# The last half of a decoder kernel: token pairs through the feed-forward one by one, hidden units on partitions

## The chip, the cores and the metric

The kernel runs on one core of a Trainium2 chip. The metric is the device time of one execution in microseconds (us); "before" is the median of three runs, 2210.0 us (2209.04 to 2211.79). The engines are named as the profile names them: PE multiplies matrices (PEld is its loading of weights), DVE and ACT work element by element and can read PE's result memory PSUM, [...]and SP, ACT and POOL have queues on which they issue DMAs.

## The reference

One decoder layer on x of 4 x 1024 tokens x 512 features, all in float32: a gated self-attention within the sequence, a cross-attention to a context of 4 x 1024 x 384, and a feed-forward, each behind a layer norm and added to x. What the change touches is the feed-forward:

```python
s = jnp.einsum('btd,dm->btm', x, Win) + bin_            # 512 -> 64 channels
h = jax.nn.relu(s[..., None] * W1 + b1)                 # 16 hidden units for each channel
g = jnp.einsum('btmh,mh->btm', h, W2) + b2              # back to 64
out = jnp.einsum('btm,md->btd', g, Wout) + bout         # 64 -> 512
...
x = x + _L0_ffn_ref(_layernorm(x, axis=-1), ...)
```

Each of the 64 channels has a small network of its own with 16 hidden units.

## The kernel before

The work is cut into units: a phase (self-attention, then cross-attention) times a batch row, eight units in order, and each unit into two halves of 512 tokens, that is four tiles of 128 tokens. `attention(u, hf)` gives the 32 score steps of a half (four groups of heads times eight tiles of keys): PE forms scores in PSUM (L574), ACT exponentiates (L579), DVE adds up for the denominators (L587), PE multiplies with the values (L601). `beside(u, hf)` gives the list of other work, and `run` deals it out between the score steps by the weights written beside each part. So the order of instructions on every engine is written out by hand; the only things decided elsewhere are the waits between engines.

The other work for a half comes from `post(u, hf)`: output projection (`project`, L87 through the helper `columns`, which makes four products of 32 columns each that fill the array side by side), residual add (L770), layer norm (`root`, `norm`), and, in the second phase, the feed-forward. There the normalized rows are turned so that features lie on partitions, multiplied with Win (`inputs`, L841), and then `hidden(h)` goes through the 16 hidden units: the 64 channels of the first two tiles (pair 0) lie on partitions 0 to 63, those of the other two (pair 1) on partitions 64 to 127, and for each unit ACT makes one relu of 128 x 256 (L858) and DVE one multiply-and-add into g (L864). `outputs(t)` multiplies with Wout (L875), adds the residual on DVE (L881) and stores a tile (L883).

The feed-forward of a half is dealt out beside the attention of the next one. The last half of the last unit has no next one. Its work, and the rest of the half before it, stand behind the loop in an order of their own: `settle` makes the last denominators on PE and divides (L719, L720), the projection's parts come as `o[0]` to `o[7]` (`o[2t]` three quarters of tile t, `o[2t+1]` the last quarter), and

```python
go(o[1], o[3], *o[4:6], *sum(held[0]["out"], []), ln[0], *ln[2:4], *o[6:8], b[0], *tr[0:2], s[0])
go(ln[1], *ln[4:6], b[1], *tr[2:4], s[1])
...
h = sum(tail["h"], [])
go(*h[0:4])
...
go(*h[4:], *sum(tail["out"], []))
```

`held[0]["out"]` are the outputs of the half before, `ln` roots and norms, `tr` the turning of a tile by PE (`across`, L325), `s[k]` the product with Win for a pair, `b` (L892) puts the bias bout into PSUM ahead of the outputs, and `h` are the 16 hidden units. PSUM is shared out by pools: `bank()` has two buffers of one bank (f), the score tiles s two of two banks, and av and sm are one bank each. Weights of 1 MB live in three buffers (w), the exponentiated tiles in six (e). A flag that says whether the fast path was numerically safe is computed from `marks` (L723, L724, L1063 to L1070); at the end each engine reads it (L59) and branches.

## Time and profile before

| | us |
|---|---|
| median of the runs before | 2210.0 |
| the profiled execution, its own time | 2212.4 |
| its span, first to last instruction | 2210.6 |
| last score product of the loop | about 2151 |
| last add on DVE ends | 2204.6 |
| last store's issue ends | 2204.95 |

| engine | busy us | share |
|---|---|---|
| PE | 2174.1 | 98% |
| DVE | 1562.2 | 71% |
| ACT | 1238.5 | 56% |
| POOL | 82.0 | 4% |

In the lines that follow in the prediction, a line of the chain has the start, the duration, the engine, what it writes and the source line; a line of the timeline has start and duration, engine, line, operation, what is written from what, shapes and count, and in brackets how long the engine stood idle before and what ended that. In the table of stretches come the stretch and its length, busy time and number of instructions of PE, PEld, DVE, ACT and POOL, then the clock granted to PE, the share of the DMA engines and GB/s. A float32 product appears as two records.

### The profile page before, as it was taken

To read this page: it belongs to the slowest core of one execution; us is meant where nothing else is said; L and a number is where in the kernel's file an instruction comes from. 1 tells how busy PE (TensorE), PEld (TensorE's weight loads), DVE (VectorE), ACT (ScalarE), POOL (GpSimd) and SP (SyncE) were. 2 spreads that over 40 slices of the span, in tenths; PEclk is the share of its full clock that TensorE was granted. 3 is DMA by queue.
4 is the path that set the end of the run, shared out by engine and by line. 5 is a ranking of instruction groups with operands and counts; after the bars stand their busy time and mean duration, and the time that the engine had idled before them with its cause. 6 is when DMAs were issued, how large, how long until landed. Compare 5 with 4: busy or idle time off the path is not lost.

```text
span 2210.6 us, 52746 instructions
## 1 busy us (share of the span) xinstructions
PE 2174.1 (98%) x22598; PEld 547.7 (25%) x22598; DVE 1562.2 (71%) x2526; ACT 1238.5 (56%) x1489; POOL 82.0 (4%) x118
## 2 busy tenths in 40 slices
PE   8999999999999999999999999999999999999995
PEld 3322222222222222222222222222222222222222
DVE  4478675796757957577686666877787777856476
ACT  0155545555455554555556565676757566667673
POOL 1000000030300000000000000000000000000000
PEclk9999999999999999999999999999999999999998
DMA  4412123032230211211232132312233142303031
GB/s 142 132 56 63 55 98 106 24 88 66 100 106 25 85 66 55 79 37 51 60 89 89 45 87 64 101 60 65 58 98 87 60 97 64 88 12 117 21 88 40
DMA packets 153304, 161.70 MB, mean 73 GB/s; under 512 B 46202, under 2 KB 91898, under 8 KB 151908
## 3 DMA queue, kind: packets, MB, share of 16 engines
q1 hardware_dynamic: 149068, 156.14, 24.4%
q8 instruction: 179, 2.93, 0.6%
q0 software_dynamic: 2144, 0.98, 0.3%
q10 hardware_dynamic: 1848, 1.12, 0.2%
q14 instruction: 65, 0.53, 0.1%
HBM read 115.40 MB, written 42.74 MB: 72 GB/s over the span
## 4 chain that ended last, share of the span: by engine, by line
PE 92%; DVE 3%; issue 2%; DMA 2%; ACT 2%; SPq 0%; DVEq 0%; ACTq 0%
PE f L87 35%; PE s L574 24%; PE av L601 21%; PE sm L609 6%; PE sm L631 3%; DVE es L587 1%; ACT e L579 1%; PE f L875 1%; DMA xn<-rows_d 1%; DVE g L864 1%; PE f L841 1%; DMA rows_d<-r 0%; PE f L325 0%; PE f L471 0%; PE f L1025 0%
## 5 line engine op out<-in xcount | busy, mean ns | idle before, releaser
L579 ACT ACTIVATE e<-s 128x1024 f32<-128x1024 f32 x1024 | 993.7, 1022 | 713.2 <-PE s L574 518.0
L587 DVE TENSOR_TENSOR es<-es,e 128x1024 f32<-128x1024 f32 x534 | 642.3, 1227 | 255.8 <-ACT e L579 253.5
L574 PE MATMUL s<-q,k 32*64 32x512 f32 x8192 | 608.7, 614 | 4.5 <-ACT e L579 2.9
L601 PE MATMUL av<-e,v 128*32 128x512 f32 x4096 | 551.1, 604 | 0.0
L87 PE MATMUL f<-xT,w 128*32 128x512 f32 x2816 | 333.7, 592 | 0.6 <-PE f L87 0.6
L595 DVE SCALAR_TENSOR_TENSOR eg<-e,sw,eg 128x512 f32<-128x512 f32 x448 | 318.6, 747 | 2.3
L585 DVE TENSOR_TENSOR es<-e 128x1024 f32<-128x1024 f32 x89 | 106.7, 1222 | 221.0 <-ACT e L579 187.8
L574 PEld LDWEIGHTS s<-q,k 32*64 32x64 f32 x8192 | 133.1, 130 | 449.4 <-ACT e L579 243.3
L87 PE MATMUL f<-w,q 128*32 128x512 f32 x1984 | 240.5, 592 | 0.7 <-DVE q L720 0.7
L601 PEld LDWEIGHTS av<-e,v 128*32 128x32 f32 x4096 | 88.1, 108 | 404.6 <-issue 401.4
L87 PEld LDWEIGHTS f<-xT,w 128*32 128x32 f32 x2816 | 92.1, 110 | 211.3 <-issue 204.4
L609 PE MATMUL sm<-e,sw 128*2 128x512 f32 x1024 | 133.3, 592 | 0.0
L87 PE MATMUL f<-w,xT 128*32 128x512 f32 x896 | 106.0, 592 | 0.6 <-DVE q L284 0.6
L87 PEld LDWEIGHTS f<-w,q 128*32 128x32 f32 x1984 | 65.5, 110 | 150.0 <-issue 142.3
L858 ACT ACTIVATE hid<-sT,units 128x256 f32<-128x256 f32 x128 | 76.7, 605 | 31.1 <-DVE g L864 24.5
L87 PE MATMUL f<-w,ctxT 128*32 128x512 f32 x768 | 92.6, 592 | 0.0
L87 PE MATMUL f<-ctxT,w 128*32 128x512 f32 x768 | 92.3, 592 | 0.0
L778 POOL TENSOR_TENSOR r<-res,bo_bc 128x512 f32<-128x512 f32 x32 | 40.9, 1278 | 1040.5 <-DVE res L770 702.7
L631 PE MATMUL sm<-es,ones 128*1 128x512 f32 x348 | 65.8, 601 | 0.0
L864 DVE SCALAR_TENSOR_TENSOR g<-hid,units,g 128x256 f32<-128x256 f32 x120 | 57.7, 481 | 11.3 <-ACT hid L858 5.8
L770 DVE TENSOR_TENSOR res<-f,res 128x512 f32<-128x512 f32 x62 | 42.5, 686 | 17.9 <-PE f L87 8.9
L681 DVE TENSOR_TENSOR q<-both,recb 128x512 f32<-128x512 f32 x63 | 43.3, 687 | 7.5 <-DMA recb<-rec_d 7.5
(258 smaller groups left out, 1037.2 us busy)
## 6 DMA issues: line engine op xcount, KB each, us to landing
recb<-rec_d SPq DMA_DIRECT2D x252, 64.0 KB
xT<-rows_d SPq DMA_DIRECT2D x60, 256.0 KB
rows_d<-r SPq DMA_DIRECT2D x60, 256.0 KB
w<-in_xattn_Wo SPq DMA_DIRECT2D x9, 1024.0 KB
w<-wout_d SPq DMA_DIRECT2D x8, 1024.0 KB
res<-in_x SPq DMA_DIRECT2D x32, 256.0 KB
x1b_d<-r SPq DMA_DIRECT2D x32, 256.0 KB
res<-x1b_d SPq DMA_DIRECT2D x32, 256.0 KB
```

Of the source, the lines that this page charges most:

```text
L87: nc.tensor.matmul(to[r], lhsT=lhsT[:, j, :] if len(lhsT.shape) == 3 else lhsT[:, r], rhs=rhs, **flags)
L574: nc.tensor.matmul(s[m : m + 64, j, :], lhsT=k[r, g, kt * P + m : kt * P + m + 64], rhs=q[r, g, :], start=True, stop=True,)
L579: nc.scalar.activation(e, s, AF.Exp, scale=SCALE)
L585: nc.vector.tensor_tensor(me["es"][i], me["e", 0][i], es[i], ALU.add)
L587: nc.vector.tensor_tensor(me["es"][i], me["es"][i], es[i], ALU.add)
L595: nc.vector.scalar_tensor_tensor(eg, es[0][:, h, :], gate(kt), eg, ALU.mult, ALU.add)
L601: nc.tensor.matmul(av[r, :], lhsT=me["v"][:, kt, HG * g + h, :], rhs=es[h // 2][:, h % 2, :], start=(kt == 0), stop=(kt == NT - 1),)
L609: nc.tensor.matmul(sm[j * DH : j * DH + sums, :], lhsT=me["sw"][:, t, HG * g + 2 + h, :] if ph == 0 else ones, rhs=me["e", t][1][:, h, :], ...
L631: nc.tensor.matmul(sm[j * DH : j * DH + 1, :], lhsT=ones, rhs=e, start=True, stop=True)
L681: nc.vector.tensor_tensor(me["q", hf][:, g, :], both[:, 0, :], all_, ALU.mult)
L858: nc.scalar.activation(hid, res["s"], AF.Relu, bias=units[:, 1, h : h + 1], scale=units[:, 0, h : h + 1])
L864: nc.vector.scalar_tensor_tensor(res["g"], res["hid"], units[:, 2, h - 1 : h], res["g"], ALU.mult, ALU.add)
```

## The change

In the last half of the last unit the feed-forward is done for pair 0 and then for pair 1, with hidden units on partitions. There are 64 x 16 = 1024 of them, eight chunks of 128. A constant 0/1 matrix "spread" copies each channel to its 16 units by a product on PE (four products of 32 x 64 per pair of chunks, 256 columns), ACT or DVE applies w1, b1 and relu with per-partition operands (the first chunk of each two on ACT, the second on DVE in two passes, except in the last two, both on ACT), and a matrix "gather" with W2 folded in adds the 16 units up again on PE, into av for pair 0 and into sm for pair 1. The matrices are loaded into a weight buffer by four DMAs beside the first half of the last unit (`load_spread`), and W2 is folded in by one DVE pass beside the second half (`fold_w2`).

Besides, in the last half the residual enters the projection through PE, as a product with the identity (`keep`) ahead of the others; ACT then copies the sum to SBUF, and the statistics read PSUM. The outputs of the half before (`kept`) get their residual in the same way, and ACT copies them out. The bias bout is added to the rows on POOL, and no longer put into PSUM by products. A pair's outputs are two tiles: the first with an identity product and an ACT copy, stored from ACT's queue, the second with a DVE add, stored from SP's. The order behind the loop is written anew.

```diff
+        def load_spread():
+
+            w = wp.tile([P, NC, D], F32, tag="w", name="w").rearrange("p c d -> p (c d)")
+            k = NF * P
+            S["spread"] = w[:, 0:k].rearrange("p (c i) -> p c i", c=NF)
+            S["gather"] = w[:, k : k + NF * M].rearrange("p (c m) -> p c m", c=NF)
+            S["hidden"] = w[:, k + NF * M : k + NF * M + 3 * NF].rearrange("p (w c) -> p w c", w=3)
+            for i in range(2):
+                nc.sync.dma_start(S["spread"][i * M : (i + 1) * M], a["spread"])
+            nc.sync.dma_start(S["gather"], a["gather"])
+            nc.sync.dma_start(S["hidden"], a["units"])
+
+        def fold_w2():
+            w2 = S["hidden"][:, 2, :].unsqueeze(2).to_broadcast([P, NF, M])
+            nc.vector.tensor_tensor(S["gather"], S["gather"], w2, ALU.mult)
+
+        def networks(res, k, g):
+
+            nk = NF // 2
+            r = slice(k * M, (k + 1) * M)
+            cols = slice(0, 2 * P)
+            hid = {}
+
+            def spread(i):
+
+                s = ps.tile([P, 2, HALF], F32, tag="s", name="s")
+                for j in range(2):
+                    c, rows = i + nk * j, slice(k * M + j * DH, k * M + (j + 1) * DH)
+                    for m in range(0, P, 64):
+                        nc.tensor.matmul(
+                            s[m : m + 64, j, cols], lhsT=S["spread"][rows, c, m : m + 64], rhs=res["s"][rows, :],
+                            start=True, stop=True,
+                        )
+                for j in range(2):
+                    c = i + nk * j
+                    hid[c] = p4.tile([P, 2, HALF], F32, tag="e", name="e", bufs=6)[:, 0, cols]
+                    w1, b1 = (S["hidden"][:, w, c : c + 1] for w in range(2))
+                    if j and i < nk - 1:
+                        nc.vector.tensor_scalar(hid[c], s[:, j, cols], w1, b1, ALU.mult, ALU.add)
+                        nc.vector.tensor_scalar(hid[c], hid[c], 0.0, None, ALU.max)
+                    else:
+                        nc.scalar.activation(hid[c], s[:, j, cols], AF.Relu, bias=b1, scale=w1)
+
+            def gather(i):
+                for j in range(2):
+                    nc.tensor.matmul(
+                        g[k * M + j * DH : k * M + (j + 1) * DH, cols], lhsT=S["gather"][:, i + nk * j, ts(j, DH)],
+                        rhs=hid[i + nk * j], start=(i == 0), stop=(i == nk - 1),
+                    )
+
+            def summed():
+                nc.scalar.activation(res["g"][r, :], g[r, cols], AF.Identity, bias=fb[r, 1:2])
+
+            return spread, gather, summed
...
+            kept = (u, hf) == (len(order) - 1, 0)
...
+            def keep(t, to):
+
+                nc.tensor.matmul(to, lhsT=ident, rhs=res[t], start=True, stop=False)
...
+                            if cs[0] == 0:
+                                keep(t, res["po"])
                         for c in cs:
                             columns(
                                 res["po"], me["q", hf][:, c, ts(t, P)], me["wo", hf][:, c, :],
-                                start=(c == 0), stop=(c == NC - 1),
+                                start=(c == 0 and not last), stop=(c == NC - 1),
...
-                        r = res[t]
-                        nc.vector.tensor_tensor(r, res["po"], r, ALU.add)
+                        r = res["po"] if last else res[t]
+                        if last:
+                            nc.scalar.copy(res[t], r)
+                        else:
+                            nc.vector.tensor_tensor(r, res["po"], r, ALU.add)
...
-                if not res.get("banks"):
-                    two = ps.tile([P, 2, HALF], F32, tag="s", name="s")
-                    res["banks"] = [two[:, i, :] for i in range(2)]
-                return res["banks"].pop(0)
+                return ps.tile([P, 2, HALF], F32, tag="s", name="s")[:, 0, :]
...
-                return lambda: nc.vector.tensor_tensor(res[t], res[t], bout_bc, ALU.add)
+                return lambda: (nc.gpsimd if last else nc.vector).tensor_tensor(res[t], res[t], bout_bc, ALU.add)
...
+            def pair_inputs(k):
+
+                def f():
+                    if k == 0:
+                        res["s"] = p2.tile([P, 2 * P], F32, tag="sT", name="sT", bufs=1)
+                        res["g"] = p2.tile([P, 2 * P], F32, tag="g", name="g", bufs=1)
+                    ss = bank()
+                    r = slice(k * M, (k + 1) * M)
+                    for c in range(NC):
+                        for m in range(2):
+                            nc.tensor.matmul(
+                                ss[k * M + m * DH : k * M + (m + 1) * DH, 0 : 2 * P],
+                                lhsT=win[:, c, m * DH : (m + 1) * DH], rhs=chunk(res["xn"], c, 2 * k, 2),
+                                start=(c == 0), stop=(c == NC - 1),
+                            )
+                    nc.scalar.activation(res["s"][r, :], ss[r, 0 : 2 * P], AF.Identity, bias=fb[r, 0:1])
+                return f
...
-                    po = res["bout", t] if last else [bank(), bank()]
+                    po = [bank(), bank()]
+                    for k in range(2):
+                        if kept:
+                            keep(2 * k + t, po[k])
                     for k in range(2):
                         nc.tensor.matmul(
                             po[k], lhsT=res["g"][k * M : (k + 1) * M, ts(t, P)], rhs=wout[k * M : (k + 1) * M, :],
-                            start=not last, stop=True,
+                            start=not kept, stop=True,
                         )
                     for k in range(2):
                         i = 2 * k + t
-                        nc.vector.tensor_tensor(res[i], po[k], res[i], ALU.add)
+                        if kept:
+                            nc.scalar.copy(res[i], po[k])
+                        else:
+                            nc.vector.tensor_tensor(res[i], po[k], res[i], ALU.add)
                         tt = 4 * hf + i
                         nc.sync.dma_start(out[b][tt * P : (tt + 1) * P, :], res[i])
...
-            def bout(t):
-
-                def f():
-                    po = res["bout", t] = [behind(), behind()]
-                    for k in range(2):
-                        r = slice(k * M, (k + 1) * M)
-                        nc.tensor.matmul(
-                            po[k], lhsT=share[r].to_broadcast([M, P]), rhs=bout_bc[r, :], start=True, stop=False
-                        )
-                return f
+            def pair_outputs(k):
+
+                two = ps.tile([P, 2, HALF], F32, tag="s", name="s")
+                r = slice(k * M, (k + 1) * M)
+                keep(2 * k, two[:, 0, :])
+                for t in range(2):
+                    nc.tensor.matmul(
+                        two[:, t, :], lhsT=res["g"][r, ts(t, P)], rhs=wout[r, :], start=t == 1, stop=True
+                    )
+                nc.scalar.copy(res[2 * k], two[:, 0, :])
+                nc.vector.tensor_tensor(res[2 * k + 1], two[:, 1, :], res[2 * k + 1], ALU.add)
+                for t, dma in enumerate((nc.scalar.dma_start, nc.sync.dma_start)):
+                    tt = 4 * hf + 2 * k + t
+                    dma(out[b][tt * P : (tt + 1) * P, :], res[2 * k + t])
...
+            if last:
+                r |= {"res": res, "outputs": pair_outputs}
...
-                "b": [[(2, bout(t))] for t in range(2)] if last else [[(0, biased(t))] for t in range(4)],
+                "b": [[(0, biased(t))] for t in range(4)],
                 "tr": [[(1 if last else 0, tr(t))] for t in range(4)],
-                "s": [[(2, inputs)]] if not last else [[(1, lambda k=k: inputs((k,)))] for k in range(2)],
+                "s": [[(2, inputs)]] if not last else [[(1, pair_inputs(k))] for k in range(2)],
...
+                else:
+                    out += one(load_spread)
                 out += pause(2) + weave(h[0:k], pause(10)) + weave(h[k:], last["o"]) + held.pop()["out"]
                 out += (ending[0]["load"] if hf else []) + weave(last["ln"], pause(5)) + last["xT"]
                 out += weave(last["b"], pause(8))
-                out += weave(last["tr"], pause(3)) + last["s"] + weave(some(last, 8), pause(14))
+                out += (one(fold_w2) if hf else []) + weave(last["tr"], pause(3)) + last["s"] + weave(some(last, 8), pause(14))
...
-        go(o[2], *h[0:3])
+        go(o[2], *h[0:3], o[4])
         for t in range(4):
             divide(t)
             go(*h[3 + 2 * t : 5 + 2 * t])
         S[n - 1]["divided", 1] = HG - 1
-        go(o[1], o[3], *o[4:6], *sum(held[0]["out"], []), ln[0], *ln[2:4], *o[6:8], b[0], *tr[0:2], s[0])
-        go(ln[1], *ln[4:6], b[1], *tr[2:4], s[1])
-
+        go(o[1], o[6], o[3], ln[0], o[5], o[7], *sum(held[0]["out"], []), *ln[2:4], *tr[0:2], s[0])
+        go(ln[1], *ln[4:6], *b)
+        spread, gather, summed = networks(tail["res"], 0, av)
+        spread(0)
+        spread(1)
+        go(tr[2])
+        gather(0)
+        spread(2)
+        go(tr[3])
+        gather(1)
+        spread(3)
+        gather(2)
+        gather(3)
+        summed()
 
         look()
         fine = p1.tile([P, 2 * NS + B * NT], F32, name="fine")
         nc.vector.tensor_scalar(fine, marks, LIM, None, ALU.is_le)
         least = p1.tile([P, 1], F32, name="least")
         nc.vector.tensor_reduce(least, fine, AX.X, ALU.min)
+        go(s[1])
+        tail["outputs"](0)
+        spread, gather, summed = networks(tail["res"], 1, sm)
+        spread(0)
+        spread(1)
+        gather(0)
+        spread(2)
+        gather(1)
+        spread(3)
         pn = bank()
         nc.tensor.matmul(pn[0:1, 0:1], lhsT=least, rhs=ones, start=True, stop=True)
-        h = sum(tail["h"], [])
-        go(*h[0:4])
+        gather(2)
+        gather(3)
+        summed()
         nc.vector.tensor_scalar(flag, pn[0:1, 0:1], P - 0.5, None, ALU.is_lt)
-        go(*h[4:], *sum(tail["out"], []))
+        tail["outputs"](1)
 
```

More of the change, by code (lines that the diff above doesn't have):

```diff
@@ L832, in tr, with inputs @@
                 return f if last else lambda: blocks(res["xn"], t)
-            def inputs(ks=(0, 1)):
-                if 0 in ks:
-                    res["ss"] = bank()
-                ss = res["ss"]
+            def inputs():
+                ss = bank()
                 for c in range(NC):
-                    for j in range(2 * ks[0], 2 * ks[-1] + 2):
+                    for j in range(4):
                         k, m = divmod(j, 2)
@@ L845, in inputs @@
                         )
-                if 1 not in ks:
-                    return
                 sT = p2.tile([P, 2 * P], F32, tag="sT", name="sT", bufs=1)
@@ L851, in inputs @@
                 res["g"] = p2.tile([P, 2 * P], F32, tag="g", name="g", bufs=1)
+            def pair_inputs(k):
[3 more added lines that the diff above has]
+                        res["g"] = p2.tile([P, 2 * P], F32, tag="g", name="g", bufs=1)
+                    ss = bank()
+                    r = slice(k * M, (k + 1) * M)
[8 more added lines that the diff above has]
+                return f
             def hidden(h):
```

## The prediction

> **What bounds the kernel now.** I read the page first:
>
> ```profile
> PE 2174.1 (98%) x22598; PEld 547.7 (25%) x22598; DVE 1562.2 (71%) x2526; ACT 1238.5 (56%) x1489; POOL 82.0 (4%) x118
> ```
>
> PE carries the kernel, but the change leaves the attention loop alone but for five instructions. What it rewrites comes after the last score step, from about 2150 us to the end at 2210.6. So I asked for the chain of waits of that stretch:
>
> ```profile
> 2168.22 0.59 DVE res L881
> 2168.81 0.04 issue
> 2168.85 2.67 PE f L875 x4
> 2171.52 5.55 PE s L87 x32
> 2177.07 1.06 PE s L892 x4
> 2178.12 1.93 PE f L325 x64
> ...
> 2180.77 1.92 PE f L841 x16
> ```
>
> The last half is a relay of single steps: a projection of the fourth tile that waits in the queue until 2171.5, four transposes, the 512-to-64 products. Then the timeline of the end:
>
> ```profile
> 2189.87 9.36 ACT L858 ACTIVATE hid<-sT,units 128x256 f32<-128x256 f32 x16
> 2192.22 7.55 DVE L864 SCALAR_TENSOR_TENSOR g<-hid,units,g 128x256 f32<-128x256 f32 x13
> 2199.82 3.44 PE L875 MATMUL s<-wout,g 64*128 64x512 f32 x8 [10.41 <-DVE g L864]
> 2201.95 2.65 DVE L881 TENSOR_TENSOR res<-s,res 128x512 f32<-128x512 f32 x4 [2.18 <-PE s L875]
> 2202.66 2.29 SPq L883 DMA_DIRECT2D out<-res  x4
> ```
>
> Sixteen hidden units go through ACT and DVE for both pairs at once (to 2199.8), then four products, four adds, four stores. Last, the busy time by stretches, whose third number from the right is the granted PE clock:
>
> ```profile
> 2165.30:2168.70 3.40, 1.16 (x3) 0.29 (x2) 3.26 (x7) 0.00 (x0) 0.18 (x1) 0.99 0.00 0
> 2168.70:2172.10 3.40, 3.25 (x8) 1.20 (x12) 1.83 (x4) 0.00 (x0) 0.00 (x0) 0.50 0.42 154
> 2172.10:2175.50 3.40, 3.40 (x20) 0.79 (x16) 2.63 (x15) 0.77 (x1) 0.00 (x0) 0.50 0.43 157
> 2175.50:2178.90 3.40, 3.40 (x52) 1.39 (x48) 1.66 (x4) 0.04 (x1) 0.06 (x1) 1.00 0.02 5
> 2199.40:2202.70 3.30, 2.88 (x8) 1.19 (x8) 1.12 (x3) 0.00 (x0) 0.00 (x0) 0.50 0.04 10
> ```
>
> After a stretch with 1.16 us of PE work the clock is halved for two stretches, and again at the end.
>
> **What the Trainium skill says.** "TensorE: Matmul & The Clock Gate", Part 1, has PE at half clock after an idle window of about 3.4 us and at full clock after a busy one; the lines above agree (2168.7 to 2175.5 is 6.8 us, two windows). It doesn't say how much work counts as busy; the trace only puts it between 1.16 us of 3.4 (fell) and 2.50 (held, 2182.3 to 2185.7). "PSUM — Partial Sum Buffer", PSUM bank collisions, says that ACT and DVE mayn't read one bank together. Before shows no such pair, but the changed program has DVE's statistics, and DVE's add of a pair's second tile, wait for ACT's copy. "ScalarE: Activation LUTs", What ACT_TABLE_LOAD costs, adds 93 ns for each per-partition operand.
>
> **Prices, from rows.** A group of four 32-column products of 512 columns 0.86 us (weights reload every 0.43 per two); a full 128x128x512 product 0.86 (3.7 us for the four of L233); 256 columns 0.43; a tile's transpose 0.9. From PE's last column to the reader 0.25 (two transposes start 2178.05, their first copy 2179.20). ACT copy from PSUM of 512 0.59, of 256 0.37; normalizing 0.81. Two operands onto 0.37 give an estimate of 0.56 for a relu from PSUM; bounds 0.37 and 0.605 (L858). DVE statistics 0.69+0.18, root 2.5, add 0.69. DVE's two-step relu isn't in the trace: 0.42 (L862's 0.41) plus 0.34 (L1063, 160 columns in 0.245, scaled); bounds 0.25 and 0.48 each.
>
> **The change, part by part**, in before's clock times, PE at full speed.
>
> *In the loop.* Four more loads on SP (about 0.55 us each, 2.2) after 1923.7; SP's next work is at 1938.7, so idle time covers them; without it the denominators behind would be 2 us late. Folding W2 is one DVE pass (0.69) at about 2123, beside DVE's waits of 0.54 and 1.71 for DMAs. Uncovered, 0.7. Both zero; range 0 to +0.7.
>
> *Projection.* Residuals now enter through PE: four identity products more (3.4 us), for which DVE loses four adds. From 2151.2 PE has 17 groups + 4 = 21 x 0.86 and ends at 2169.2; the second tile is 19th, out at 2167.8. Divisions end at 2163.6 as before, since sums stand one product later (about 2155.75) but DVE only comes to them at 2155.84. Copy 0.59, statistics 1.0, root 2.5: 2171.9, against 2174.7 before. Statistics of two more tiles (1.9) and the norm (0.54): 2174.4. The second root ends at 2176.9, before 2181.4. The idle stretch is gone, and with it the half clock there.
>
> *First half's outputs*, now in front of the transposes on PE and ACT. Two identity products and a concurrent pair (3 x 0.86): 2171.8; two ACT copies to 2173.35. The next two identities want those banks: pair out at 2175.4, copies to 2176.9. Queued behind them on ACT is the second tile's norm (0.81): 2177.7. Transpose 1.15, copy 0.59, products 1.97: 2181.6, bias copy 2182.1. Before's products ended at 2182.7. So the first pair's head is only 1.3 ahead: most of the 4 us won is lost to this ping-pong.
>
> *First pair's network.* ACT first does the fourth tile's norm (0.81), then relus at 2182.97 and 2183.57; DVE may start after each (0.76 a unit). Spread, gather, transposes and relus alternate with 0.25 at each hand-over; last relu 2188.5, last gather 2189.2, sum 2189.75. PE is free for the second pair's products (1.72+0.25) at 2189.0: 2191.0, bias copy 2191.5. Before had it at 2189.83, so the second pair is 1.6 late.
>
> *First pair's outputs.* Identity, then two products of one row group, one after the other: 2190.7 to 2193.3. Copy 2194.2, the ACT store's issue 0.5, DVE add 2194.9. The second pair's second spread needs that buffer: queued behind it is PE. It starts at 2195.0; ACT's first relu waits for the issue (2194.8).
>
> *Second pair.* Spread 0.68, relu 0.56, DVE 0.76, gather 0.43, spread 0.68, relu 0.56, DVE 0.76 or two relus 1.2, gather 0.68, with gaps: 2200.2. Sum 0.46: 2200.7. Two products 1.97: 2202.8; copy 2203.4; add 2204.2. Removed for it: the 16 relus and sums (10.3 us), the half-clock products (3.44) and two of four adds.
>
> *POOL's* four bias adds (1.28 each, L778) end near 2184.3; the first is wanted at 2190.7 and the others later, so hidden.
>
> *End.* Before: last add 2204.6, SP's last issue 2204.95, flag load, branch, and
>
> ```profile
> L60 SPq EVENT_SEMAPHORE  x8: 17/17/17, 2208.3 to 2208.9; - x8
> ```
>
> that is, 5.65 us from the issue to the end, with the stored data through at 2206.3. Two stores instead of four in the end, on two queues, save issues that were already hidden behind adds ("DMA: Bandwidth & Descriptors", Issuing engines are not separate DMA queues, says only issue time is saved). I take the same 5.65.
>
> Sum: last add 2204.2 for 2204.6, so -0.4 us: 2210.2 for the span of 2210.6. That execution took 2212.4 in all, above the median 2210.0 of the runs; taken from the median it is **2209.6**. Measurement cannot tell less than about 0.2% (4.4 us) from no change.
>
> **Rivals.** *A: about the same* (0.65), the sum above, own range 2207 to 2212.5: with 0.1 instead of 0.25 at the hand-overs it loses 1.3 more; with DVE's and ACT's new passes at their upper bounds, some 0.1 each on about ten steps, it gains 1.
>
> *B: the clock falls in the second pair* (0.18). PE there runs 0.43 us pieces with waits between, often a quarter of the array: about 2.1 us in 3.4, between the two measured stretches. If it halves from 2193 to 2196, all later pieces double: the two last products alone cost 1.7, all together 4.7, hence 2214; at 2199, 3.0. So 2212 to 2214.5.
>
> *C: slower* (0.10). The same mechanism one stage earlier: between 2175.7 and 2182 PE has 1.8 to 2.5 us of work per window. If it falls there or at the latest by 2190, the first pair's outputs run at half clock too and nothing after is dense enough to restore it: +7.2, 2217. By 2190 is the point from which it passes 0.2%. Against it: 2.50 and 2.65 us held the clock in before.
>
> *D: faster* (0.07). Short hand-overs (-1.3), DVE and ACT passes at their lower bounds (about -1.5), and an earlier landing of the shorter store backlog (-1): 2206 or a little below. For it, nothing but the bounds; against it, the 0.25 is seen in three places.
>
> **Numbers.** Faster by over 0.2% (below 2205.6): D and A's edge, 0.09. Slower (above 2214.4): C, a third of B, and an unpriced wait in A, 0.19. The rest, 0.72. Leaving out C and the outer edge of D, the range is 2205.5 to 2215.
>
> **What would show it.** Right: sixteen-unit ACT rows gone; no half clock between 2168 and 2175; first sum's bias copy near 2182, the second near 2191.5; the last add near 2204. Wrong: a halved clock after 2176; DVE's statistics late because ACT's copies queue; the four spread tiles running one after another (0.43 each, +2); recb or the first sums late.

## The result, and the profile after

The changed kernel takes 2214.1 us (median of 22 executions, 2211.5 to 2218.1); the kernel before 2210.7 us (22 executions, 2208.1 to 2213.2). The ratio is 1.0015, with a 95% interval from 1.0009 to 1.0021: 3.4 us slower, where 0.4 faster was forecast. The prediction held that less than 0.2% can't be told from no change; with 22 executions on each side the interval is 0.12% wide and lies clear of 1. The profiled execution took 2215.0 us, its span is 2213.2.

The engines' busy times in that execution:

```profile
PE 2187.5 (99%) x22706; PEld 552.5 (25%) x22706; DVE 1554.5 (70%) x2513; ACT 1241.3 (56%) x1496; POOL 87.5 (4%) x122
```

PE is busy for 13 us more than before. The question is which of these 13 us lie on the path to the end. The chain of waits of the last half (start, duration, engine, what it writes, line):

```profile
2163.73 1.72 PE s L87 x16
2165.45 0.90 PE f L87 x8
2166.37 0.59 ACT res L833
...
2175.34 0.58 ACT res L961
2175.92 0.72 ACT xn L872
...
2178.53 1.95 PE f L921 x16
...
2194.79 1.54 PE sm L773 x4
```

Up to 2166.4 PE's projection is on the path, where before it was the divides and the adds. Then, as forecast, ACT's copies of the first half's outputs (L961) hold up the norm of the second tile (L872), and the products with Win (L921) wait for that. The last line is a gather, two products of 256 columns (four records); its sister in the first network takes 0.77. The timeline of that stretch shows that other products are slow there too (brackets: idle before, and what ended it):

```profile
2196.26 1.13 PE L757 MATMUL s<-sT,w 32*64 32x256 f32 x8
2197.45 0.56 ACT L769 ACTIVATE e<-s,w 128x256 f32<-128x256 f32 x1 [2.04 <-PE s L757]
2205.59 0.69 DVE L978 TENSOR_TENSOR res<-s,res 128x512 f32<-128x512 f32 x1 [5.84 <-ACT res L977]
2206.31 0.33 SPq L981 DMA_DIRECT2D out<-res  x1
```

A spread takes 1.13 us here and 0.66 in the first network, and ACT sits idle for 2.04 us until it ends. Busy time by stretches, cut at the edges of the clock's windows (third number from the right: granted PE clock):

```profile
2167.82:2171.23 3.41, 3.17 (x12) 0.98 (x8) 2.93 (x17) 0.74 (x2) 0.19 (x1) 1.00 0.00 0
2191.71:2195.13 3.42, 2.49 (x21) 0.61 (x19) 1.45 (x3) 1.43 (x3) 0.00 (x0) 1.00 0.25 95
2195.13:2198.54 3.41, 3.41 (x19) 0.90 (x22) 1.41 (x4) 0.85 (x2) 0.00 (x0) 0.50 0.15 58
```

The half clock at 2168.7 is gone, as forecast; in its place the clock falls at 2195.13, in the second network, and comes back at 2201.95. The prediction took it that one busy window brings the full clock back; here PE was busy in all 3.41 us of the window from 2195.13, and the next window was still at half. Last, the end of the program:

```profile
L60 SPq EVENT_SEMAPHORE  x8: 17/17/17, 2210.9 to 2211.5; - x8
L60 ACTq EVENT_SEMAPHORE  x1: 17/17/17, 2210.8 to 2210.8; - x1
```

SP goes on right after ACT has come out of its branch, at 2210.8. Before, ACT was through with that at 2201.7.

**Where the time went, stage by stage.** All experiments below were profiled too, and in units of these stages their traces agree to 0.1 us wherever nothing was changed and the clock was the same, except in the last stage: it takes 6.0 us in e2 and 6.7 in e11, whose tails have the same instructions. So one table serves for all. The stages: from the start of the last score product (L574) to the end of the last divide (L720); from there to the end of the first pair's bias copy (into sT); to the second pair's; to the end of the last add on DVE; to the end of the span. In the kernel before, one copy serves both pairs, so its 26.27 spans two columns. The kernels e2 to e10 are described below. "Predicted" is the prediction's own timetable, counted from before's last score product at 2148.52.

| us | to last divide | to first bias copy | to second | to last add | to the end | sum | clock in the tail |
|---|---|---|---|---|---|---|---|
| before | 15.05 | (both pairs) | 26.27 | 14.77 | 5.97 | 62.05 | halved twice |
| predicted | 15.05 | 18.5 | 9.4 | 12.7 | 6.0 | 61.7 | full |
| after | 15.71 | 19.80 | 9.19 | 16.13 | 6.90 | 67.73 | halved at 2195 |
| e3, both stores on SP | 15.70 | 19.80 | 9.19 | 13.76 | 6.08 | 64.53 | full to the last product |
| e2, residual by DVE | 15.03 | 15.68 | 9.18 | 13.73 | 6.00 | 59.63 | full |
| e10, interleaved | 15.71 | 19.80 | 9.19 | 11.97 | 6.90 | 63.57 | full |
| e9, both | 15.04 | 15.69 | 9.19 | 11.96 | 6.81 | 58.69 | full |

The tail of this one execution is 5.7 us longer than before's, yet the span grew by only 2.6. The other 3.1 lie ahead of it: before's last score product starts at 2148.52, after's at 2145.45, and e5 and e6 below show that this is no gain of the change.

### The profile page after: what moved, and what is told of

Same layout as the page of the kernel before. It is cut to its first block, busy times and chain, and to the rows that moved or that the text cites. A ratio compares the mean times of both kernels' runs of the same rounds, so it can differ in the third digit from the quotient of the medians.

```text
span 2213.2 us, 52969 instructions
## 1 busy us (share of the span) xinstructions
PE 2187.5 (99%) x22706; PEld 552.5 (25%) x22706; DVE 1554.5 (70%) x2513; ACT 1241.3 (56%) x1496; POOL 87.5 (4%) x122
## 4 chain that ended last, share of the span: by engine, by line
PE 94%; DVE 2%; ACT 1%; DMA 1%; issue 1%; SPq 0%; DVEq 0%; ACTq 0%
PE f L87 36%; PE s L574 25%; PE av L601 21%; PE sm L609 6%; PE sm L631 3%; ACT e L579 1%; DVE es L587 1%; PE f L954 1%; PE f L901 0%; DMA xn<-rows_d 0%; PE f L325 0%; PE f L471 0%; DMA rows_d<-r 0%; DMA sum_d<-both 0%; PE s L87 0%
## 5 line engine op out<-in xcount | busy, mean ns | idle before, releaser
L574 PE MATMUL s<-q,k 32*64 32x512 f32 x8192 | 607.3, 613 | 4.7 <-ACT e L579 3.2
L601 PE MATMUL av<-e,v 128*32 128x512 f32 x4096 | 550.2, 603 | 0.0
L87 PE MATMUL f<-xT,w 128*32 128x512 f32 x2816 | 333.7, 592 | 0.5 <-PE f L87 0.5
L574 PEld LDWEIGHTS s<-q,k 32*64 32x64 f32 x8192 | 132.8, 129 | 448.4 <-ACT e L579 244.0
L87 PE MATMUL f<-w,q 128*32 128x512 f32 x1984 | 239.2, 592 | 0.0
L601 PEld LDWEIGHTS av<-e,v 128*32 128x32 f32 x4096 | 87.9, 108 | 403.9 <-issue 401.3
L87 PEld LDWEIGHTS f<-xT,w 128*32 128x32 f32 x2816 | 92.1, 110 | 211.2 <-issue 204.7
L87 PE MATMUL f<-w,xT 128*32 128x512 f32 x896 | 106.0, 592 | 0.6 <-DVE q L284 0.6
L87 PEld LDWEIGHTS f<-w,q 128*32 128x32 f32 x1984 | 64.4, 110 | 150.1 <-issue 143.7
L87 PE MATMUL f<-w,ctxT 128*32 128x512 f32 x768 | 92.6, 592 | 0.0
L87 PE MATMUL f<-ctxT,w 128*32 128x512 f32 x768 | 92.3, 592 | 0.0
L934 ACT ACTIVATE hid<-sT,units 128x256 f32<-128x256 f32 x112 | 67.4, 606 | 31.5 <-DVE g L940 25.1
L940 DVE SCALAR_TENSOR_TENSOR g<-hid,units,g 128x256 f32<-128x256 f32 x105 | 50.4, 480 | 9.7 <-ACT hid L934 5.8
```

The lines of the kernel that those rows point to most:

```text
L87: nc.tensor.matmul(to[r], lhsT=lhsT[:, j, :] if len(lhsT.shape) == 3 else lhsT[:, r], rhs=rhs, **flags)
L574: nc.tensor.matmul(s[m : m + 64, j, :], lhsT=k[r, g, kt * P + m : kt * P + m + 64], rhs=q[r, g, :], start=True, stop=True,)
L601: nc.tensor.matmul(av[r, :], lhsT=me["v"][:, kt, HG * g + h, :], rhs=es[h // 2][:, h % 2, :], start=(kt == 0), stop=(kt == NT - 1),)
L934: nc.scalar.activation(hid, res["s"], AF.Relu, bias=units[:, 1, h : h + 1], scale=units[:, 0, h : h + 1])
L940: nc.vector.scalar_tensor_tensor(res["g"], res["hid"], units[:, 2, h - 1 : h], res["g"], ALU.mult, ALU.add)
```

## The experiments

The medians of the kernel before in the three groups of runs were 2210.8, 2210.3 and 2210.9. Times are medians; ratios are against the kernel before in the same group. The groups ran on different chips, so between groups the ratios are the fairer measure.

**First group: one part each.** *e1: keep the clock up in the second network.*

```diff
+        def fill(n):
+            nc.tensor.matmul(av[:, 0:n], lhsT=ident, rhs=tail["res"]["xn"][:, 0, 0:n], start=True, stop=True)
         spread(0)
+        fill(512)
         spread(1)
+        fill(256)
         gather(0)
...
```

> The changed kernel with products that nobody reads put on PE in the second pair's network (one of 512 columns where PE waits for DVE's add, then 256 columns ahead of each of the first three gathers); the result is unchanged. Theory 'the clock fell': the half clock from 2195.1 to 2201.9 is gone, the second network takes 5.7 to 6.1 us instead of 8.1, the kernel 2211.6 (-2.0 to -2.8 against 2214.1). Rival 'ACT and DVE set the pace of the relay': PE's clock is full and the time stays at 2214 or rises by up to 0.5.

Measured: 2215.75 us (1.0019, interval 1.0010 to 1.0028); in the profile, which is of the fastest of the 12 executions (2213.0), the clock is full to 2205.6 and the second network takes 6.5 us (2194.37 to 2200.91). The clock did what the theory said, the time didn't: a dummy product of 256 columns takes 0.63 us on the chain. From second bias copy to last add it is 14.50 us, against 16.13 with a fall and 13.76 in e3 without one. So dummies are no cure, and the fall must be priced in another way.

*e3: both stores of a pair from SP's queue.*

```diff
-                for t, dma in enumerate((nc.scalar.dma_start, nc.sync.dma_start)):
+                for t, dma in enumerate((nc.sync.dma_start, nc.sync.dma_start)):
```

> The changed kernel, but both tiles of a pair are stored from SP's queue. Theory 'ACT's last issue makes its branch and the fetch after it the last thing to end': ACT is released 0.4 us earlier, and from SP's last issue to the end it takes 5.7 to 6.2 us instead of 6.55; the kernel 2213.2 to 2213.7. Rival 'the landing of the last store sets it': no difference, 2214.1.

Measured: 2214.86 us (1.0016, 1.0010 to 1.0023). In the profile the end is 6.08 us after the last add, instead of 6.90, but the time doesn't show it. What this run gave instead is a tail in which the clock happened not to fall, with nothing added to PE. Here is its stretch in the second network, to compare with the second line of stretches above:

```profile
2196.58:2199.99 3.41, 2.48 (x26) 0.96 (x24) 2.27 (x5) 1.57 (x4) 0.00 (x0) 1.00 0.40 154
```

With 2.48 us of PE work in 3.41 the clock stays up in the next two stretches; after 2.49 us it fell. The work is the same, but the edges lie elsewhere against it: this stretch begins 3.0 us after the second bias copy, the other 1.6 us. "TensorE: Matmul & The Clock Gate", Part 1, says that the windows run free and don't start with the kernel; the traces agree, with all edges of a trace at multiples of 3.413 us from each other, and their place against the program another one in each profile. So it looks as if the position of the windows in an execution decides whether the clock falls in this stretch; e6 below has executions of both kinds. The fall costs 16.13 - 13.76 = 2.37 us. The queue has no part in this difference, since e2, with two queues and no fall, has 13.73; in e6's profile the fall came elsewhere against the work and cost 2.0 (15.77).

*e2: the residual of the last half by DVE, as before the change.*

```diff
-                            if cs[0] == 0:
-                                keep(t, res["po"])
...
-                        r = res["po"] if last else res[t]
-                        if last:
-                            nc.scalar.copy(res[t], r)
-                        else:
-                            nc.vector.tensor_tensor(r, res["po"], r, ALU.add)
+                        r = res[t]
+                        nc.vector.tensor_tensor(r, res["po"], r, ALU.add)
```

> The changed kernel, but in the last half the residual is added by DVE after the projection, as before the change, not by an identity product on PE. Theory 'the identity products of 1.05 us each are paid in full': PE ends the projection near 2164 instead of 2168, the first root ends 2 to 3 us earlier, the kernel 2211.5 (-2 to -3). Rival 'they fill a hole in which the clock would fall': PE stands idle for over 2 us between 2164 and 2169, the clock is halved for 6.8 us as in the kernel before, and the time is 2214 to 2217.

Measured: 2210.65 us (0.9998, 0.9989 to 1.0006), 3.5 less than the changed kernel. The profile is of the fastest of the 13 executions (2206.5), so it is read by stages and not by its total. No fall comes back at 2168. In the table the first two stages are 0.68 and 4.12 us shorter, 4.8 in all, for four products priced at 3.4. PE at the start of the projection and behind its end, first the changed kernel:

```profile
2147.28 1.38 PE L601 MATMUL av<-e,v 128*32 128x512 f32 x6
2148.59 1.13 PE L811 MATMUL f<-res,ident 128*128 128x512 f32 x2
2149.64 2.78 PE L87 MATMUL f<-w,q 128*32 128x512 f32 x24
2152.24 1.04 PE L713 MATMUL sm<-es,ones 128*32 128x512 f32 x8
...
2167.95 1.98 PE L811 MATMUL f<-res,ident 128*128 128x512 f32 x4
```

and the same place with the residual on DVE:

```profile
2146.48 1.36 PE L601 MATMUL av<-e,v 128*32 128x512 f32 x6
2147.34 0.60 PE L87 MATMUL f<-w,q 128*32 128x512 f32 x2
2147.68 0.60 PE L601 MATMUL av<-e,v 128*32 128x512 f32 x2
...
2149.91 0.60 PE L713 MATMUL sm<-es,ones 128*32 128x512 f32 x2
...
2162.80 1.98 PE L811 MATMUL f<-res,ident 128*128 128x512 f32 x4
```

Without the identity product, the first 32-column products of the projection (L87) start 0.34 us ahead of the last of the products with the values (L601): the four strips of 32 columns work side by side, and one is already free. With it, L601 ends in all four first, the 128-column product runs alone for 1.05 us, and only then does L87 begin. The last score product starts at 2145.45 in the one, at 2145.08 in the other; from there L87 begins 4.19 us later in the first and 2.26 in the second. So the first product, of 0.86 us, costs 1.93. "TensorEngine Tiling (Array Packing)", Key Properties, says that changing the tiling mode drains the engine, without a price; this trace agrees, and the price is 1.07 us above the product's own time. The sums (L713) are late by as much, and the divides with them by 0.68. The last line of each fence is what PE does when the projection is over, the identity products of the half before: 22.50 us after the last score product in the first, 17.72 in the second. So the four products cost PE 4.78 us. In e2 PE works without a break from the last score product to there, and its chain of waits runs along PE all the way, so the whole of the saving is PE's time.

*e4: the hidden units as before, everything else as changed.*

```diff
-        spread, gather, summed = networks(tail["res"], 0, av)
...
+        go(*tr[2:4], s[1])
...
+        go(*h[4:])
         tail["outputs"](0)
         tail["outputs"](1)
```

> The changed kernel with its head (residual through PE, order of the projection, first half's outputs early, a pair's outputs as changed), but the feed-forward's hidden units as before the change: the second pair's transposes and products directly after the first pair's, then sixteen relus for both pairs at once. Theory 'the head won, and the relay of two networks gave it back': the second pair's bias copy ends near 2185, sixteen relus of 0.605 us end near 2195, two pairs of outputs at half clock end near 2201.5; the kernel 2209 to 2210. Rival 'the head won nothing': the bias copy ends near 2189 as before, and the time is 2213 to 2216.

Measured: 2216.64 us (1.0026, 1.0017 to 1.0036): the theory missed. The second pair's bias copy does end 4.15 us earlier than in the changed kernel (24.84 us after the divides, not 28.99; before 26.27), but from there to the last add it takes 20.95 us. Sixteen relus leave PE idle, the clock falls at 2192.6, and a pair's outputs, one product of 64 rows after another, never raise it again. The stretch of the outputs, here (first fence) and in the kernel before, where two such products run side by side (second fence):

```profile
2199.42:2202.83 3.41, 3.41 (x5) 1.07 (x4) 0.00 (x0) 0.59 (x1) 0.00 (x0) 0.50 0.02 5
```

```profile
2199.37:2202.79 3.42, 2.97 (x8) 1.19 (x8) 1.24 (x3) 0.00 (x0) 0.00 (x0) 0.50 0.04 10
```

Before's clock is full after 2202.79; in e4 it stays at half to the end of the span, 22.7 us, although PE was busy in all of the stretch and of the next. So this run compares outputs more than networks, and e7 was made.

**Second group: the falls, and the head.** The head is all that the change does ahead of the hidden units. *e7: the head alone, with before's outputs too* (two tiles side by side, in two banks, DVE's adds). Against e4:

```diff
-        go(*h[4:])
-        tail["outputs"](0)
-        tail["outputs"](1)
+        go(*h[4:], *sum(tail["out"], []))
```

> The changed kernel's head alone (residual through PE, order of the projection, first half's outputs early, bias on POOL): the sixteen hidden units for both pairs at once and the outputs of two tiles side by side with DVE's adds, as before the change. Theory 'the networks bring little': the second pair's bias copy ends 1.5 us earlier than before and what follows is as before, 2209 to 2210. Rival 'the head loses and the networks win': 2213 to 2216.5, as with old units and the new outputs (2216.6).

Measured: 2211.72 us (1.0004, 0.9996 to 1.0012), between the kernels before and after. The head by itself does win: the second pair's bias copy ends 24.84 us after the divides against 26.27, so 1.4 us earlier, about what the prediction gave the first pair's; but the divides are 0.65 later. The stage to the last add then takes 16.38 us instead of 14.77: with two banks in place of before's four, the second tiles' products wait 0.84 us for DVE's adds, and the clock, which fell at 2193.0, stays at half to the end. So neither head nor networks is worth much alone.

*e5 and e6: PE fed at 1931 us, in the kernel before and in the changed one.* Before's profile had one more half clock, which the prediction passed over. Its stretches there:

```profile
1929.72:1933.13 3.41, 1.40 (x16) 0.16 (x8) 2.31 (x4) 1.97 (x3) 0.00 (x0) 1.00 0.01 2
1933.13:1936.55 3.42, 3.25 (x20) 0.71 (x24) 0.00 (x0) 3.21 (x6) 0.00 (x0) 0.50 0.00 0
```

PE waits 2.17 us for ACT's exponential, which stands behind a hidden unit that waits for DVE. In the changed kernel's profile the same wait falls across an edge (1932.30), and the clock holds, after a window with less PE work than the one that fell at 2195.13:

```profile
1928.89:1932.30 3.41, 1.89 (x24) 0.17 (x10) 2.79 (x5) 1.49 (x3) 0.00 (x0) 1.00 0.61 141
```

So PE's busy time in a window does not decide alone. Two products that nobody reads were put ahead of the wait:

```diff
+        def fill_stall():
+            idle = bank()
+            for _ in range(2):
+                nc.tensor.matmul(idle, lhsT=ident, rhs=bout_bc, start=True, stop=True)
...
+                    out += one(fill_stall)
```

> The kernel before with two products of 128x128x512 that nobody reads, put on PE just ahead of its 2.17 us wait at 1931 us; the result is unchanged. Theory 'the clock falls there in nearly every execution of the kernel before' (its profile lost 2.7 us there, and the mean clock of its runs leaves room for no other reading): 2208.0, that is -2.3 to -2.9 against 2210.8. Rival 'it falls in about half of them, by the phase of the windows': -1.0 to -1.6. Rival 'another wait takes the time': 0.

> The changed kernel with the same two products at 1931 us; the result is unchanged. Theory 'the two kernels are alike up to 2140 us': the gain is the same as that of the kernel before with them, whatever it is. Rival 'the changed kernel doesn't fall there' (its profile doesn't): 0, it stays at 2214.1, and then 2 to 3 us of the loss were hidden in the comparison.

Measured: before 2208.79 (0.9994, 0.9985 to 1.0002), after 2212.43 (1.0013, 1.0006 to 1.0019): -1.5 and -1.7. The two kernels are alike up to the tail: with the wait filled, the last score product starts at 2145.73 and 2144.99, and in all the profiles without a fall there it starts between 2144.5 and 2146.1. The fall costs 2.8 us where it comes (2148.52 against 2145.73), and gains of 1.5 and 1.7 fit with a fall in about half of the executions, in both kernels; that it comes in nearly all is not borne out. So the comparison of medians is fair, but that of two profiles is not: before's had this fall, after's hadn't. With the wait filled on both sides the change still costs 3.6 us.

e6 also prices the other fall. Ten of its 21 executions had a mean granted clock of 0.999, and took 2211.2 to 2212.3 us; six had 0.997, and took 2213.6 to 2215.3. The medians of these two sets, 2211.8 and 2214.4, differ by about the 2.4 us of the half clock in the second network; the five with 0.998 lie between, at 2212.4 to 2214.7. The profiled execution is one of the six, with a fall at 2193.8 after 2.48 us of PE work in the window. Without that fall, then, the change would still cost 3.0 us (2211.8 against e5's 2208.8).

*e8: the holes filled with work.* The residual by DVE (e2), the products of e6, and the order behind the first pair's network written anew: its outputs go to two banks of `bank()`, and the second pair's first two spreads stand between its identity product and the other two (the cut below). At the end, the last identity product goes ahead of the last gather, and the flag is set behind the last add.

```diff
-                two = ps.tile([P, 2, HALF], F32, tag="s", name="s")
+                po = po or [bank(), bank()]
                 r = slice(k * M, (k + 1) * M)
-                keep(2 * k, two[:, 0, :])
+                keep(2 * k, po[0])
+                between()
                 for t in range(2):
...
-        tail["outputs"](0)
...
+        po = tail["products"](0, lambda: (spread(0), spread(1)))
         gather(0)
+        tail["store"](0, po)
```

> The changed kernel with the residual added by DVE after the projection (2210.7 alone), the two products at 1931 us, and the second pair's first two spreads put between the first pair's identity product and its output products, which go to two single banks; a tile's identity product at the end is put ahead of the last gather. Theory 'the relay waits, and what stands in its holes is free': the second network starts near 3 us earlier after its bias copy, PE has no hole there in which the clock falls, 2204 to 2206.5. Rival 'ACT and DVE set the relay's pace whatever PE does between': 2209 to 2211.

Measured: 2206.29 us (0.9980, 0.9973 to 0.9986), faster than the kernel before. All 21 executions have a mean clock of 0.998 or 0.999. Its end takes 7.23 us from the last add: with the flag's last step on DVE behind that add, all five engines branched together at 2199.4, and the last of them was through at 2203.6.

**Third group: do the parts add?** *e9: e8 with the flag where it was*, ahead of the last pair's outputs, and the last identity product behind the last gather again (the cut is against e8). *e10: the same, with the residual by PE. e11: e2 with e6's products. e12: e9 with both stores on SP.*

```diff
+        gather(3)
+        summed()
+        nc.vector.tensor_scalar(flag, pn[0:1, 0:1], P - 0.5, None, ALU.is_lt)
         two = ps.tile([P, 2, HALF], F32, tag="s", name="s")
-        po = tail["products"](1, lambda: (gather(3), summed()), [two[:, i, :] for i in range(2)])
-        tail["store"](1, po)
-        nc.vector.tensor_scalar(flag, pn[0:1, 0:1], P - 0.5, None, ALU.is_lt)
+        tail["store"](1, tail["products"](1, lambda: None, [two[:, i, :] for i in range(2)]))
```

> As the interleaved kernel (2206.3), but the flag is set by DVE before the last pair's outputs, as in the changed kernel, and not after the last add, and the last identity product stands again behind the last gather. Theory 'at the end each engine's branch and the fetch after it count, and set late they all come last': from the last add to the end 6.0 to 6.5 us instead of 7.2, the kernel 2205.0 to 2205.8. Rival 'the landing of the store sets the end': 2206.3.

> The changed kernel with the two products at 1931 us (2212.4) and the second pair's spreads between the first pair's output products, the residual of the last half through PE as in the changed kernel. Theory 'the falls and the holes of the second network are one part of the loss, the identity products in the projection another, and they add': no half clock in the tail, the last add 1.5 to 3 us earlier, the kernel 2209 to 2210. Rival 'what was gained came with the residual on DVE alone': 2212.

> The changed kernel with the two products at 1931 us (2212.4) and the residual of the last half by DVE. Theory 'the four identity products cost what their time on PE is, 4 x 1.05 less the copies': 2208.0 to 2209.0, still with the clock falling in the second network in some executions. Rival 'the residual's gain was the missing fall at 1933 us in its executions': 2210.5 to 2212.

> As the first kernel of this group, but with both tiles of a pair stored from SP's queue, where no fall of the clock blurs the time. Theory 'ACT's issue at the end delays ACT's branch and fetch': 0.4 to 0.8 us less than with two queues. Rival 'the queues make no difference': within 0.2 us of it.

| median, us (ratio to before) | relay as changed | interleaved |
|---|---|---|
| residual by PE | e6: 2212.4 (1.0013) | e10: 2210.6 (0.9999, 0.9990 to 1.0007) |
| residual by DVE | e11: 2208.65 (0.9987, 0.9980 to 0.9993) | e9: 2204.8 (0.9973, 0.9962 to 0.9984) |

All four with PE fed at 1931 us. In the profiles the parts add to a few hundredths: the residual by DVE is worth 4.8 us (first two stages, e10 against e9), interleaving 1.76 (13.72 to 11.96 from the second bias copy to the last add, in e11 and e9, both at full clock), and it keeps the clock up besides (all 20 executions of e9 and e10 at 0.999; e11 has 0.997 to 0.999), which is worth about 1.2 on average if half of the executions fall. The ratios say 0.0026 (5.7 us) for the residual in both columns of the table and 0.0014 (3.1 us) for interleaving in both rows; each ratio has an interval of 1.4 to 2.4 us either way. The medians, with e6 from another chip, say 3.8 and 5.8 for the first and 1.8 and 3.9 for the second. The traces' 4.8, and 1.76 with the 1.2, lie within these intervals. The end of e9 against e8 also shows what the place of the last identity product is worth: ahead of the last gather it made the stage to the last add 12.49 us, behind it 11.96. PE's relay in e9:

```profile
2184.50 1.13 PE L811 MATMUL f<-res,ident 128*128 128x512 f32 x2
2185.55 1.09 PE L757 MATMUL s<-sT,w 32*64 32x256 f32 x16
2186.57 1.98 PE L970 MATMUL f<-wout,g 64*128 64x512 f32 x4
2188.49 0.63 PE L773 MATMUL sm<-e,w 128*32 128x256 f32 x4
```

Both spreads are done before the output products of the pair before, which fill the time that ACT and DVE need for their four passes; in the changed kernel PE did the outputs first, and the second spread then waited 0.93 us for DVE's add to free its buffer.

e12: 2205.17 us (0.9974, 0.9964 to 0.9984), the same as e9. Its profile again has a shorter end (6.14 us after the last add; e9 6.81), as e3 had. The times don't follow, twice, so the queues are not shown to matter. e9 is 4.0 us below the kernel before with the same products (e5), 4.6 by the ratios, so the plan of the change was sound once two of its steps were mended.

## Why the prediction was wrong, point by point

It said 2209.6 us and "about the same"; 2214.1 is inside its range and just within the 0.2% bound, but slower, where it forecast a little faster. That the median lands on rival B's 2214 is luck: B gets there with a fall of 4.7 us alone, while the measured loss is the identity products' and a fall of 2.4 us in about half of the executions. The step that failed is the residual through PE: the four identity products were priced at 3.4 us and taken to pay for themselves, and they cost 4.8. By its own steps:

- **The loop** (four loads and a fold, zero): right, e5 and e6 agree up to the tail within what profiles of one stretch differ by.
- **The base.** It worked against the profile of before and took that execution's excess over the median off. It looked for half clocks only behind 2165, and so left out the one at 1933, which had cost that execution 2.8 us. This cost the forecast nothing, but made the two profiles look 3.1 us closer than their tails are.
- **"Projection. ... four identity products more (3.4 us) ... 21 x 0.86": this step failed.** The price was that of a product among its like (the four of L233); between column-tiled products the first took 1.93, and all four cost PE 4.78 (e2). "Divisions end ... as before, since sums stand one product later": the sums came 1.95 us later, past the slack, and the divides 0.66. Together with the 1.3 in the next stage the timetable is 2.0 us short. That DVE "loses four adds" was right and worth nothing, for DVE waited there. So the move of the residual, which was taken to pay for itself, costs 4.8 us: e2 takes it back and has them.
- **The idle stretch and its half clock gone**: right; but they are gone without the identity products as well, in e2's profile and in all seven executions of e9 (clock 0.999).
- **First half's outputs ping-pong**: right in order and mechanism (the chain above). Its steps add up to 2181.4 us, not 2181.6.
- **First pair's network** (9.4 us to the second bias copy): right, 9.19. DVE's two steps took 0.54 and 0.29 for the estimated 0.42 and 0.34 (the first is outside its bound of 0.48), ACT's relu 0.56 as estimated.
- **First pair's outputs, second pair**: 12.7 us forecast, 13.76 at full clock (e3), so 1.06 too few. Against the timetable, e3's second spread starts 0.47 us late, the network to the end of its sum adds 0.16, and the last output products, which wait for an identity product of 1.05 us behind the last gather, add 0.35; 0.08 come after. The steps listed for the network add up to 5.0 us and leave only 0.2 of its 5.2 for hand-overs priced at 0.25 each, so that it came out nearly right is no proof of the list. Then **rival B**: 16.13. Its mechanism was named. Its place and price less so: its timetable has the last score product at 2148.52, 3.07 us later than this profile, so the fall at 2195.1 would stand there at 2198.2, near its case "at 2199, 3.0", and it cost 2.4. The chance of 0.18 was too low for something that came in about half of the executions of e6. It was set from PE's busy time between two measured stretches (1.16 us fell, 2.50 held); windows with 2.49 that fell and with 1.89 that held show that busy time alone doesn't decide.
- **End** (5.65 us from SP's last issue): 6.55 in this profile. ACT, which had long been through its branch in before, now issues the second-last store and is the last to come out ahead of SP. From the last add the profiles have 5.9 to 6.1 us for kernels whose last stores all go out on SP, and 6.0 to 6.9 for those with two queues and an early flag. Whether the times feel it stays open (e3, e12).

The sum for this execution: 0.66 + 1.30 - 0.21 + 1.06 + 2.37 + 0.90 = 6.08 us above the predicted tail of 61.7 (measured 67.73). Less the 3.1 us by which the loop ended earlier, that is the 3.0 between the 2210.2 forecast for the span and its 2213.2. Rival A's mechanism was right in the main, and two of its prices were wrong; rival C (the clock falling by 2190) came in no profile of a kernel with the two networks, and rival D's bounds were not reached by any step.

What stays open: which work counts for the clock; the queues at the end; and moving the second pair of the first half's outputs out of the head, which wasn't tried.

## What to carry to other kernels

Price an added product by what stands beside it: here a full-array product between column-tiled ones cost 1.93 us at its first place for the 0.86 that it takes among its like, and a DVE add off the path was the cheaper place. In a relay between engines, try to put the next link's first products ahead of the last link's output products: here the same work then filled the hole, where dummies lengthened the chain, and the clock held. Before forecasting tenths of a per cent from one profile, look through the whole of it for half clocks, since the same program can have one in one execution and none in the next (e6).

## What was not expected of the hardware

- A 128-column identity product among 32-column ones: 1.93 us instead of 0.86 for the first, and 4.78 us of PE's time for four (after, e2).
- The clock fell after a stretch with 2.49 us of PE busy in 3.42 (after) and after one with 2.48 (e6), and held after one with 2.48 (e3) and one with 1.89 (after, at 1932.3). In e1's profile, with full-array dummies in that stretch, it held. At half clock, 3.41 of 3.41 us of PE work, mostly 64-row products one by one, didn't bring it back (e4); 2.97 us of the same products two by two did (before), and 2.56 us of them did not (e7).
- DVE's L293 on 2 columns, 0.17 us elsewhere, took 1.11 at 2172.85, while POOL's bias add ran (2172.67, 1.27 us). It recurs in e2 on L293 and L298 (1.12 and 1.27), each time beside a bias add. It was off the path here, but POOL's adds had been priced as hidden altogether.
- Flag set late, all engines branching at once: 7.23 us from the last add to the end, against 6.81 with it early (e8, e9; one profile each, and kernels with it early range from 6.0 to 6.9).
